# Storing one group of x1 in two cuts, with the first loads of the next stage between them

## The chip, the core and the metric

The kernel runs on one core of one Trainium2 chip, in one launch. The metric is the device time of that launch in microseconds (us), as the median of several runs. The engines of the core are named as in the profile: PE (TensorE), DVE (VectorE), ACT (ScalarE), POOL (GpSimd) and SP (SyncE). In this kernel SP does no arithmetic; it issues nearly all the transfers between the chip's memory and the on-chip memory.

## What is computed

The input x has 8 elements (B) of 8 channels, each 512 x 512 in float32. Two layers are applied, each with a residual. Cut to what matters:

```
# layer 0
x1 = x + spectral(gn(x))          # 2D Fourier modes of the subsampled x, 8 by 4 of them, mixed over channels
# layer 1
v   = gn(x1)                      # mean and variance over groups of 2 channels
cml = v                           # 15 steps of a lattice map
repeat 15 times:
    m   = 3.9 * cml * (1 - cml)
    cml = 0.85 * (0.7 * m + 0.3 * conv3x3_per_channel(m)) + 0.15 * v
cml = clip(cml, 1e-4, 1 - 1e-4)
nca = sigmoid(conv1x1(relu(conv3x3(v, 128 hidden))))
g   = sigmoid(conv1x1(relu(conv3x3([v, cml, nca], 8))))
out = x1 + g * cml + (1 - g) * nca
```

## The kernel before, in words

For every element the kernel keeps three planes in the chip's memory: `xn` (the normalised x1), `cml` and `nca`, with rows outermost and the 8 channels of a row next to each other (`[row, channel, 512]`, with a row of padding at the top, so that plane row 1 is image row 0).

**Layer 0** is the generator `layer0`. Its last part goes through the channels two at a time (a group): it adds the spectral part to a tile of x (128 partitions, four image rows in each), takes the statistics, and `close` normalises both tiles of the group on DVE (L414) and stores them into `xn` (L417, one DMA of 1024 KB for a channel). The store is put off by a tick with `later`. For element 0 the store also hands the tile's place back to the pool `sets` (`done_with`), and `e.stored` counts the channels.

**Layer 1** has three kinds of work, which for elements 1 to 7 run beside layer 0 of the next element:

- the lattice steps (`Half`, `convolve` L533, `settle` L588 and L594). The image rows lie in 5 sets of four slabs; every set has one tile of input for even steps (dE) and one for odd steps (dO), loaded from `xn` in four DMAs of 256 KB each (`Half.load`, L491), scaled on POOL (L526), and a state m, which begins as a square of dE on ACT (L513);
- the hidden rounds (`Hidden`). A round is four image rows. `load` (L616) fetches `cols`, 18 rows of all channels for four rounds, in one DMA of 512 KB, with two buffers. A round is a burst of matmuls (L633), a ReLU on ACT (L639) for one half and on DVE (L641) for the other; after two rounds `point` (L652) multiplies by the second matrix, and the result is copied out of PSUM into y by ACT (L659) for the first two rounds of four, and added to y by DVE (L661) for the other two. After four rounds the sigmoid (L665) is taken and y is stored into `nca` (L668, 256 KB). There is one buffer for y;
- the gates (`Gate`), which join x1, cml and nca.

The order of all this is written out by hand: `work` emits one slot of steps and rounds, and `keep_order` fixes the order of the source on every engine. The transfers are in one queue, SP's, in the order in which they are emitted, each with a wait for what it needs.

**Around the change.** Element 0's layer 0 has nothing beside it. When it is over, `tick(end=True)` runs what was put off, and two `e.hidden.load()` calls emit the loads of the first eight rounds. Then follow eight rounds (`FIRST_ROUNDS`) in four calls of `work`, each with two rounds. The first of them emits all loads of dE and dO for which there is room (`first.fetch`), the second, after its round, the next cols and, a tick later, the store of y. After these eight rounds the first lattice steps begin.

SP's order in the prologue is thus: four stores of x1 (channels 0 to 3), 16 loads of dE and dO (sets 0 and 1), four stores (channels 4 to 7), two cols, 24 loads of dE and dO (sets 2 to 4), one cols, the store of the first y, one cols, the store of the second y. Two cols loads reach down to plane row 33, that is the first 33 image rows, which lie in partitions 0 to 8 of the tiles of x1.

Of the kernel before, what the change touches and what calls it, by code (L numbers as in the profile page):

```python
# [41 lines left out]
P = 128  # L42
C = 8
N = 512
NS = N // 2
G = 4
# [74 lines left out]
def view(t, offset, dims):  # L121

    return bass.AP(tensor=t.tensor, offset=t.offset + offset, ap=[list(d) for d in dims])
# [3 lines left out]
def conv_layers(ctx: ExitStack, tc: tile.TileContext, a, out):  # L127
    nc = tc.nc
# [39 lines left out]
    def later(ticks, work):  # L168
        put_off.append((now[0] + ticks, work))

    def tick(end=False):
        now[0] += 1
        due = [w for at, w in put_off if end or at <= now[0]]
        put_off[:] = [] if end else [(at, w) for at, w in put_off if at > now[0]]
        for work in due:
            work()
# [122 lines left out]
    def group_stats(mv, n, bank):  # L299

        mean = sm.tile([P, n], F32, name=f"mean{n}")
        ps = bank[-1][:, 0]
        nc.tensor.matmul(ps[:, :n], avg, mv[:, :, 0], start=True, stop=True)
        nc.vector.tensor_copy(mean, ps[:, :n])
        var = sm.tile([P, n], F32, name=f"var{n}")
        nc.vector.tensor_tensor(var, mv[:, :, 0], mean, ALU.subtract)
        nc.vector.tensor_tensor(var, var, var, ALU.mult)
        nc.vector.tensor_tensor(var, var, mv[:, :, 1], ALU.add)
        yield LATER
        ps = bank[-1][:, 0]  # L310
        nc.tensor.matmul(ps[:, :n], avg, var, start=True, stop=True)
        std = sm.tile([P, n], F32, name=f"std{n}")
        nc.scalar.activation(std, ps[:, :n], AF.Sqrt, bias=eps)
        rstd = sm.tile([P, n], F32, name=f"rstd{n}")
        nc.vector.reciprocal(rstd, std)
        return mean, rstd, std

    def layer0(e, bank):
# [9 lines left out]
        for c in range(C):  # L328
            yield c
            xt = e.x[c]  # L330
# [76 lines left out]
        def close(g, mv):  # L407

            mean, rstd, std = yield from group_stats(mv, 1, bank)
            nc.vector.tensor_copy(means[:, 0, g : g + 1], mean)  # L410
            nc.vector.tensor_copy(means[:, 1, g : g + 1], std)
            for c in (2 * g, 2 * g + 1):
                xt = e.x[C + c]
                nc.vector.tensor_scalar(xt, xt, mean, rstd, ALU.subtract, ALU.mult)  # L414

                def store(c=c, xt=xt):
                    nc.sync.dma_start(  # L417
                        out=e.xn[1 : N + 1, c].rearrange("(p j) w -> p j w", j=4), in_=xt
                    )
                    e.done_with(C + c)  # L420
                    e.stored += 1

                later(1, store)

        def synthesis(ty, xt, st, half):
            ps, at = bank[-1], slice(2 * half, 2 * half + 2)
# [12 lines left out]
        for c in range(C):  # L439
            yield C + c  # L440
            ty, xt = ty_next, e.x[C + c]
            if c % 2 == 0:
                st = sm.tile([P, 2, 4, 6], F32, name="st1", bufs=2)
            synthesis(ty, xt, st[:, c % 2], 0)
            if closing:
                yield LATER
                next(closing)
                yield LATER
                next(closing, None)
                closing = None  # L450
            if c + 1 < C:
                yield
                ty_next = over_rows(c + 1)
            yield LONG
            synthesis(ty, xt, st[:, c % 2], 1)
            if c % 2:
                closing = close(c // 2, aggregate(st, 1))
# [217 lines left out]
    class Gate:  # L675
# [60 lines left out]
        def store(self):  # L736
            lo = self.first - self.r0
            nc.sync.dma_start(
                out=view(
                    out, self.e.b * C * N * N + self.first * N,  # L740
                    [[N, GR - lo], [N * N, C], [1, N]],
                ),
                in_=self.mix[C * lo : GR * C, 1],
            )
            shared.drop(self.mix)
# [110 lines left out]
    for i in range(3):  # L856
        xn = dram.tile([NP + 1, C, N], F32, name=f"xn{i}")
        cml, nca = (dram.tile([NP, C, N], F32, name=f"{name}{i}") for name in ("cml", "nca"))
        for plane in (xn, cml, nca):
            nc.scalar.dma_start(  # L860
                out=view(plane, 0, [[(NP - 1) * C * N, 2], [N, C], [1, N]]), in_=zrow
# [5 lines left out]
    e = Element(0)  # L867
# [13 lines left out]
        while e.stored >= C // 2 and len(e.first.loads) > 8 * (SETS - 2) and sets.free:  # L881
            e.first.load(nc.sync)
    tick(end=True)
    e.hidden.load()
    e.hidden.load()

# [29 lines left out]
    for b in range(B):  # L918
        e = elements[b]
# [95 lines left out]
```

## Time and profile before

| | us |
|---|---|
| median of 3 runs | 9992.99 |
| the runs | 9989.27, 9992.99, 10003.49 |
| the profiled execution, its own time | 9988.58 |
| its span | 9986.8 |
| PE busy (matmul) in the span | 9359.6, 94% |
| DVE busy | 5869.1, 59% |
| ACT busy | 4297.8, 43% |
| POOL busy | 1755.5, 18% |
| mean granted clock of PE | 0.983 |

The profile is of one execution. Times within it count from the start of the span. A row of the order of time gives the start, the length, the engine and line, the operation, what it writes and reads, how many such instructions are merged into the row, and in brackets the idle time before it and what ended that. An engine name with a q (SPq) means its queue, where DMAs are issued: the length is then that of the issuing, not of the transfer. A row of busy times by stretch gives from:to, the length, the busy time of PE, PE's weight loads, DVE, ACT and POOL (with the number of instructions), the granted clock of PE, the mean busy share of the 16 DMA engines and the GB/s that they moved. A transfer that goes on beyond its own record makes such a share come out a little over 1.

### The profile page before, as it was taken

What the parts mean: (1) busy time and instruction counts of PE and PEld (TensorE: products, weight loads), DVE (VectorE), ACT (ScalarE), POOL (GpSimd) and SP (SyncE); (2) the same over time, 40 slices, a digit from 0 to 9 for tenths busy, and PEclk for the clock granted to TensorE, in tenths of its full rate; (3) what the DMA queues carried; (4) which work ended last, traced back from release to release, by engine and by line L of the source; (5) the groups of instructions that cost most, each with busy time, mean ns of one, the idle gap of its engine ahead of it and who ended that gap; (6) DMA issues with size and microseconds to landing.
All of it is one profiled execution on the core that took longest, in us unless ns stands there. A gap on an engine that the chain in (4) does not pass through costs nothing. (4 is left out here: it accounts for less than half of the span.)

```text
span 9986.8 us, 353049 instructions
## 1 busy us (share of the span) xinstructions
PE 9359.6 (94%) x160496; PEld 4296.7 (43%) x160496; DVE 5869.1 (59%) x6067; ACT 4297.8 (43%) x4445; POOL 1755.5 (18%) x1406
## 2 busy tenths in 40 slices
PE   6999999899998999989999899999999899998999
PEld 2444444443444444444444444444434444444433
DVE  5665555665566655666556655566555565555555
ACT  2444444444444434444344443444434354344422
POOL 2010111103121031101312013120121202211212
PEclk9999999999999999999999999999999999999999
DMA  4241355447544565445665356552566526753688
GB/s 147 88 120 34 82 140 134 134 127 168 139 128 136 126 163 137 133 124 135 159 144 141 112 141 162 141 158 94 143 160 145 155 91 144 168 129 94 150 199 200
DMA packets 625562, 1353.48 MB, mean 136 GB/s; under 512 B 73066, under 2 KB 73194, under 8 KB 594050
## 3 DMA queue, kind: packets, MB, share of 16 engines
q1 hardware_dynamic: 621728, 1329.77, 52.0%
q8 instruction: 1261, 20.66, 0.9%
q14 instruction: 235, 1.93, 0.1%
q10 hardware_dynamic: 2338, 1.13, 0.0%
HBM read 992.27 MB, written 268.78 MB: 126 GB/s over the span
## 5 line engine op out<-in xcount | busy, mean ns | idle before, releaser
L533 PE MATMUL pair<-m,band 32*32 32x512 f32 x115200 | 4096.7, 605 | 200.2 <-issue 96.0
L594 ACT ACTIVATE m<-m 128x1024 f32<-128x1024 f32 x2240 | 2363.7, 1055 | 2795.7 <-DVE m L588 2674.2
L533 PEld LDWEIGHTS pair<-m,band 32*32 32x32 f32 x115200 | 2262.4, 103 | 1941.3 <-issue 970.0
L633 PE MATMUL pair<-cols,w_p 32*128 32x511 f32 (+1 forms) x24576 | 2866.2, 603 | 41.4 <-DMA cols<-xn 14.2
L588 DVE SCALAR_TENSOR_TENSOR m<-pair,dO 128x1024 f32<-128x1024 f32 x1280 | 1507.2, 1219 | 1478.0 <-PE pair L533 1294.2
L633 PEld LDWEIGHTS pair<-cols,w_p 32*128 32x128 f32 x24576 | 1270.8, 186 | 1651.0 <-issue 1123.3
L588 DVE SCALAR_TENSOR_TENSOR m<-pair,dE 128x1024 f32<-128x1024 f32 x1120 | 1319.1, 1219 | 1068.6 <-PE pair L533 878.3
L641 DVE TENSOR_SCALAR h<-pair,b_p 128x1024 f32<-128x1024 f32 x1024 | 1312.9, 1283 | 810.8 <-PE pair L633 803.3
L639 ACT ACTIVATE h<-pair,b_p 128x1024 f32<-128x1024 f32 x1024 | 1140.3, 1114 | 1043.4 <-PE pair L633 1043.0
L652 PE MATMUL pair<-h,w_u 128*32 128x512 f32 x8192 | 996.5, 598 | 136.4 <-DVE h L641 123.5
L726 POOL TENSOR_TENSOR mix<-mix 96x512 f32<-96x512 f32 x344 | 437.4, 1271 | 3757.9 <-ACT mix L724 3551.2
L703 PE MATMUL pair<-gin,w_g 128*32 128x511 f32 (+1 forms) x8256 | 964.1, 600 | 33.3 <-DMA gin<-nca 17.0
L708 POOL TENSOR_TENSOR mix<-mix 96x512 f32<-96x512 f32 x344 | 443.4, 1289 | 2050.6 <-DMA mix<-nca 1340.1
L598 POOL TENSOR_SCALAR dO<-dO 128x2048 f32<-128x2048 f32 x80 | 431.9, 5410 | 1225.6 <-DVE m L588 1225.5
L652 PEld LDWEIGHTS pair<-h,w_u 128*32 128x32 f32 x8192 | 249.4, 110 | 757.1 <-issue 384.0
L703 PEld LDWEIGHTS pair<-gin,w_g 128*32 128x32 f32 x8256 | 235.3, 110 | 711.2 <-issue 472.2
L665 ACT ACTIVATE y<-y,b_u 128x512 f32<-128x512 f32 x256 | 184.7, 721 | 808.0 <-DVE y L661 807.8
L731 DVE SCALAR_TENSOR_TENSOR mix<-mix,back 96x512 f32<-96x512 f32 x344 | 335.7, 976 | 148.5 <-POOL mix L726 148.5
L659 ACT COPY y<-pair 128x512 f32<-128x512 f32 x256 | 149.7, 585 | 605.1 <-PE pair L652 482.8
L713 DVE TENSOR_SCALAR mix<-pair,b_g 128x512 f32<-128x512 f32 x344 | 258.0, 750 | 251.6 <-PE pair L703 251.4
L720 PE MATMUL pair<-mix,w_g 128*32 128x512 f32 x2064 | 356.8, 593 | 9.6 <-DVE mix L713 7.8
L526 POOL TENSOR_SCALAR dO<-dO,base 128x512 f32<-128x512 f32 x320 | 237.0, 756 | 453.8 <-DMA dO<-xn 323.0
(86 smaller groups left out, 2643.8 us busy)
## 6 DMA issues: line engine op xcount, KB each, us to landing
gin<-xn SPq DMA_DIRECT2D x344, 384.0 KB
cols<-xn SPq DMA_DIRECT2D x256, 512.0 KB
x<-in_x SPq DMA_DIRECT2D x120, 1024.0 KB
gin<-cml SPq DMA_DIRECT2D x344, 320.0 KB
gin<-nca SPq DMA_DIRECT2D x344, 320.0 KB
dE<-xn SPq DMA_DIRECT2D x320, 256.0 KB
dO<-xn SPq DMA_DIRECT2D x320, 256.0 KB
mix<-xn SPq DMA_DIRECT2D x344, 192.0 KB
```

The source lines that it names most:

```text
L533: nc.tensor.matmul(ps[h // 2][32 * t : 32 * t + 32, h % 2], band[at, c0 + (t if step % 2 else h), dx], m[at, t, dx : dx + N], start=(n == ...
L588: nc.vector.scalar_tensor_tensor(u[:, at], ps[q], FLOOR, d[:, at], ALU.max, ALU.add)
L594: nc.scalar.square(u[:, at], u[:, at])
L598: nc.gpsimd.tensor_scalar(d, d, 0.5, None, ALU.add)
L633: nc.tensor.matmul(ps[g // 2][:, g % 2, lo:hi], w_p[p, dx, i % 2], self.cols[p, i // 2, at : at + hi - lo], start=(n == 0), stop=(n == 2), ...
L639: nc.scalar.activation(h[:, :2], ps[0], AF.Relu, bias=b_p)
L641: nc.vector.tensor_scalar(h[:, 2:], ps[1], b_p, 0.0, ALU.add, ALU.max)
L652: nc.tensor.matmul(ps[32 * g : 32 * g + 32], w_u[:, r % 4], h[:, g], start=(r == self.hs[0][0]), stop=(r == self.hs[-1][0]), tile_position ...
L703: nc.tensor.matmul(ps[32 * j : 32 * j + 32, lo:hi], gband[:, dx], gin[:, j, at : at + hi - lo], start=(n == 0), stop=(n == 2), tile_positi ...
L708: nc.gpsimd.tensor_tensor(d, d, ng, ALU.subtract)
L720: nc.tensor.matmul(ps[at], gpoint[:, at], mix[:, 3], start=True, stop=True, tile_position=(0, 32 * j),)
L726: nc.gpsimd.tensor_tensor(d, d, mix[: GR * C, 2], ALU.mult)
```

## The change

The put-off store of a group is now one function for both channels. For element 0 and the last group (channels 6 and 7) the store is cut at partition 12: first partitions 0 to 11 of both channels (48 image rows each), then the two cols loads, which stood after the end of layer 0, then partitions 12 to 127 of both channels (464 image rows each). In all other cases there is one cut, so the same two DMAs as before, with the places handed back after both of them.

```diff
-                def store(c=c, xt=xt):
-                    nc.sync.dma_start(
-                        out=e.xn[1 : N + 1, c].rearrange("(p j) w -> p j w", j=4), in_=xt
-                    )
+            def store():
+
+                cuts = (0, 12, P) if not e.b and g == G - 1 else (0, P)
+                for lo, hi in zip(cuts, cuts[1:]):
+                    for c in (2 * g, 2 * g + 1):
+                        to = e.xn[1 + 4 * lo : 1 + 4 * hi, c]
+                        nc.sync.dma_start(
+                            out=to.rearrange("(p j) w -> p j w", j=4), in_=e.x[C + c][lo:hi]
+                        )
+                    if lo == 0 and hi < P:
+                        e.hidden.load()
+                        e.hidden.load()
+                for c in (2 * g, 2 * g + 1):
                     e.done_with(C + c)
                     e.stored += 1
 
-                later(1, store)
+            later(1, store)
...
     tick(end=True)
-    e.hidden.load()
-    e.hidden.load()
```

## The prediction

> **What bounds the kernel now.** I read the page first: the span is 9986.8 us and TensorE (PE) is busy 94% of it, so the kernel is bound by PE almost everywhere, but the first of the 40 slices has PE at 6 tenths. The change touches only that slice. The page's chain of waits does not reach back to it, so I read the stretch from 120 to 200 us in order of time, queue by queue. Columns are: start in us, length, engine and line, operation, tiles, count, and in brackets the idle time before it with what ended it. First the queue of SyncE (SP), which issues all the DMAs here:
>
> ```profile
> 121.74 12.07 SPq L417 DMA_DIRECT2D xn<-x  x4
> 139.87 0.92 SPq L616 DMA_DIRECT2D cols<-xn  x2
> 140.83 1.89 SPq L491 DMA_DIRECT2D dE<-xn  x4
> ...
> 162.15 3.52 SPq L491 DMA_DIRECT2D dO<-xn  x4
> 166.73 0.38 SPq L616 DMA_DIRECT2D cols<-xn  x1
> 167.84 0.34 SPq L668 DMA_DIRECT2D nca<-y  x1
> 184.25 0.36 SPq L616 DMA_DIRECT2D cols<-xn  x1
> ```
>
> The last two of the four x1 stores are issued at 131.67 and about 133.3:
>
> ```profile
> 131.67 2.14 SPq L417 DMA_DIRECT2D xn<-x  x2
> ```
>
> Then SP stands until 139.87, because the first rounds' rows (cols) read what those stores write. Behind the two cols loads come 24 loads of dE and dO, one more cols, and only then the store of y into nca. Next PE and, for one line, ScalarE (ACT):
>
> ```profile
> 143.47 7.05 PE L633 MATMUL pair<-cols,w_p 32*128 32x512 f32 x48 [14.21 <-DMA cols<-xn]
> ...
> 171.64 3.70 PE L633 MATMUL pair<-cols,w_p 32*128 32x512 f32 x28
> 178.72 5.48 PE L633 MATMUL pair<-cols,w_p 32*128 32x512 f32 x20 [3.38 <-ACT y L659]
> 185.74 3.64 PE L652 MATMUL pair<-h,w_u 128*32 128x512 f32 x16 [1.54 <-ACT m L513]
> 189.31 7.45 PE L533 MATMUL pair<-m,band 32*32 32x512 f32 x192
> ```
>
> ```profile
> 178.08 0.58 ACT L659 COPY y<-pair 128x512 f32<-128x512 f32 x1 [8.67 <-DMA nca<-y]
> ```
>
> There are two gates. One is the start of the rounds, 143.47, held by cols. The other is 178.08: y has a single buffer, so the third pair of rounds cannot be copied out until the first y has been stored, and the fourth pair needs the PSUM bank that this copy empties. The lattice steps (L533) come after it in PE's fixed order. So the second gate, not the first, sets when the steps begin, and it is a DMA landing. Is that DMA late because it is issued late or because the queue is full? The busy times by stretch (last two columns: mean busy share of the 16 DMA engines, GB/s) answer it:
>
> ```profile
> 133.00:138.00 5.00, 0.00 (x0) 0.00 (x0) 0.99 (x4) 0.00 (x0) 1.49 (x2) 1.00 1.05 408
> 139.00:141.00 2.00, 0.00 (x0) 0.00 (x0) 0.00 (x0) 0.00 (x0) 0.00 (x0) 1.00 0.08 10
> 141.00:144.00 3.00, 0.53 (x4) 0.52 (x8) 0.00 (x0) 0.00 (x0) 0.00 (x0) 1.00 0.97 334
> 145.00:165.00 20.00, 16.88 (x144) 6.56 (x140) 5.82 (x5) 7.04 (x7) 2.80 (x6) 1.00 1.04 219
> 165.00:175.00 10.00, 8.42 (x76) 3.24 (x68) 2.92 (x3) 2.23 (x2) 2.70 (x4) 1.00 1.04 225
> 739.00:742.00 3.00, 3.00 (x99) 1.67 (x102) 0.18 (x1) 2.50 (x2) 2.64 (x5) 1.00 0.83 296
> ```
>
> From 141 to 175 the DMA engines are full, apart from the hole at 139 to 141 that SP's wait leaves. The nca store is at the end of that full queue.
>
> **What the Trainium skill says.** "DMA: Bandwidth & Descriptors", section "Why a DMA increments its semaphore by 16 and not by 1": a DMA issued from SP is spread over k engines, the largest number up to 16 that divides the outermost dimension of both sides, and these are the lowest-numbered ones. The trace agrees: in the last row above the cml stores of 24 to 28 partitions (13 on average by this rule, 13/16 = 0.81) keep 0.83 of the engines busy at 296 GB/s, where the 128-partition stores keep 1.05 busy at 408. The same page, "Queues, rings and completion order": one engine takes its descriptors in the order of the ring, so what is issued later waits behind what is queued on that engine. No row of before isolates this. "TensorE: Matmul & The Clock Gate", "The HAM clock gate": after an idle window of about 3.4 us the clock drops to a half, and a busy window brings it back. The trace shows that: PEclk is 0.50 from 180 to 190 after the 3.38 us of idle.
>
> **The change, part by part.** Only SP's order in the prologue differs; elements 1 to 7 keep theirs (store, store, then release).
>
> *Small stores ahead.* Partitions 0 to 11 of the two tiles, 48 rows of 2 KB each. 12 divides both 12 and 48, so k = 12 and each engine has 4 rows. They are issued where the full stores were, 131.67 and 133.3, and the queue ahead of them (the first two stores, 2.1 MB) is through at about 133. Before, SP went on at 139.87, some 1.2 us after the stores' traffic broke off (the 2 us row of nearly nothing begins at 139). Issue to first traffic was also about 1.3 us (139.87 to 141.1). So the last small store moves at about 134.6 and SP goes on at about 136.0.
>
> *Cols moved ahead.* 136.0 instead of 139.87, then the same 3.6 us to the first matmul (139.87 to 143.47): the rounds start at about 139.6, a gain of 3.9 us. It is not worth 10 us, as the 1.9 MB that pass behind might suggest, since the DMA queue stands empty while SP waits in either order. Of this gain nothing survives if the second gate does not move: PE would stop 3.9 us earlier and wait 3.9 us longer.
>
> *Rest of the stores behind cols.* 116 partitions, 464 rows of 2 KB, twice: 1.90 MB. The largest number up to 16 that divides both 116 and 464 is 4. So these two use four engines, and the same four. One engine gives 408/16 = 25.5 GB/s (128-partition stores) or 296/13 = 22.8 (cml stores); four give 91 to 102, and 1.90 MB take 18.6 to 20.8 us instead of 4.7. With cols moving from 137.3 to 139.9 (1.05 MB at 400 GB/s), these four are taken until 158.5 to 160.7. The two extra issues on SP (0.5 us each) are hidden behind this.
>
> *What is late next.* Everything behind has a share on those four engines. In the compiled order each DMA waits for one of eight completion semaphores in turn, so six loads go out freely, the seventh when the first rest has landed (about 151), the eighth when the second has (160 to 162). The other twelve engines finish their shares of the first seven loads and then stand idle. The four then owe seven shares of 64 KB, 0.46 MB at about 100 GB/s: 4.6 us, to 163.1 to 165.3. Before, the seventh load was through at 143.7 + 7 x 1.20 = 152.1 (262 KB at 219 GB/s, starting when cols were done). That is 11.0 to 13.2 us late. From here the sequence is as before, except that the twelve are one or two loads ahead, and the four alone do a share in 0.65 instead of 1.20 us: about 1 us comes back. The nca store lands 10 to 12 us later; I take 10.5, so ACT's copy comes at 178.1 + 10.5 = 188.6.
>
> *After the gate.* The squares of dE, the driving of dO on GpSimd and the first steps need loads that landed before nca, in both orders. The clock is the part that I cannot fix: PE ran 178.7 to about 191 at half speed, 5.48 us for 20 matmuls that at the rate of the others (5.43 for 48) would take 2.26. PE idles longer now and restarts in the same cold state; one window of 3.4 us more or less is worth 1.7 us of work, two 3.4. I take nothing, and keep plus or minus 3.4. Sum: +10.5, rounded to +10 for the rounding of both ends. Against the profiled execution's own 9988.58 us (its span 9986.8 and 1.8 around it) this makes 9998.6. That execution is 4.4 below the median of the three runs, 9992.99, which I forecast from: 10003.
>
> **The rivals.**
> *Spread evenly.* If the 116-partition stores use all 16 engines, they take 4.7 us. Then the DMA work is the same in another order, and only the hole differs: before it was 139 to 141.1 plus the end of 138; now the queue is nearly empty from 133.1 to 137.3. The loads begin at 139.9 + 4.7 = 144.6 instead of 143.7: +1 us, 9994. The cml row speaks against it.
> *The gate moves with the rounds.* If the nca store lands earlier with y, the 3.9 us arrive at the end: 9989. For it: y is ready 3.9 us earlier. Against it: ACT had finished y at 164.4 and SP issued the store at 167.84, behind 16 loads, with the engines full.
> *Slower by over 0.2%.* The place is the same rest stores, but on two engines or one: two take 37 to 42 us, so the nca store lands about 29 us late, 10022; one gives some 66, 10059. It decides from a rest of about 29 us on, that is from below 2.6 engines. For it: a dimension that is carried otherwise than 116 and 464 would have other divisors. Against it: the order of the compiled program shows 464 rows on the far side, and 4 divides both.
>
> **How the numbers follow.** Four engines 0.72, 9997 to 10010 (10 to 12 by the sum, 3.4 for the clock, a few for the median of three runs that span 14 us); spread evenly 0.12, 9990 to 9998; the gate moves 0.05; over 0.2% slower 0.11. 0.2% is 20 us, about what a measurement of this kernel can tell from no change. Range 9992 to 10013. Faster by over 0.2% 0.01, within 0.87, slower 0.12.
>
> **What would show it.** In the profile after: cols issued at about 136 and PE's first round at about 139.6; a DMA share near 4/16 somewhere between 147 and 158; the dE and dO issues stretched, with two long waits for the x1 stores at 151 and 161; ACT's copy at about 188 still ended by the nca store, with PE idle some 14 to 17 us before it instead of 3.38; the first L533 at about 199. If the share stays at 1.04 through 145 to 158 and the copy comes near 179, the step with four engines is wrong. If the copy is no longer ended by the nca store, the second gate is.

## The result, and the profile after

| | before | after |
|---|---|---|
| median (20 runs each) | 9990.17 us | 10009.37 us |
| lowest to highest | 9982.74 to 10015.66 | 9989.67 to 10032.20 |
| ratio of the times, after to before, 95% interval | | 1.0016, 1.0009 to 1.0023 |
| span of the profiled execution | 9986.8 us | 9996.6 us |
| copy of the third pair of rounds (ACT) | 178.08 | 191.87 |
| first lattice step (L533 before, L542 after) | 189.31 | 201.04 |

The changed kernel is slower by 9 to 23 us. The medians are 19.2 us apart, the two profiled executions 9.8. Lines after L414 have moved down by up to 9, the hidden rounds by 9 (L633 is L642, L659 is L668).

SP's queue in order of time, after:

```profile
121.86 11.83 SPq L422 DMA_DIRECT2D xn<-x  x4
136.18 0.91 SPq L625 DMA_DIRECT2D cols<-xn  x2
137.15 6.82 SPq L422 DMA_DIRECT2D xn<-x  x2
144.01 12.78 SPq L500 DMA_DIRECT2D dE<-xn  x4
...
182.09 0.38 SPq L625 DMA_DIRECT2D cols<-xn  x1
183.27 0.34 SPq L677 DMA_DIRECT2D nca<-y  x1
```

The cols loads do go out 3.7 us earlier. But two stores take 6.82 us merely to issue, where four took about 0.5 us each before, and the 24 loads behind them end their issue some 15 us later than before (182.09 against 166.73 for the cols load that follows them). PE and the copy on ACT:

```profile
139.65 6.84 PE L642 MATMUL pair<-cols,w_p 32*128 32x512 f32 x48 [10.27 <-DMA cols<-xn]
...
192.50 5.14 PE L642 MATMUL pair<-cols,w_p 32*128 32x512 f32 x20 [21.20 <-ACT y L668]
199.19 1.92 PE L661 MATMUL pair<-h,w_u 128*32 128x512 f32 x16 [1.54 <-DVE h L650]
201.04 6.58 PE L542 MATMUL pair<-m,band 32*32 32x512 f32 x192
```

```profile
191.87 0.59 ACT L668 COPY y<-pair 128x512 f32<-128x512 f32 x1 [26.49 <-DMA nca<-y]
```

PE starts 3.8 us earlier and then stands 21.20 us instead of 3.38, at the same place and for the same reason. Busy time by stretch (the last two columns are again DMA share and GB/s):

```profile
133.00:138.00 5.00, 0.00 (x0) 0.00 (x0) 0.59 (x2) 0.00 (x0) 1.77 (x3) 1.00 0.50 126
142.00:152.00 10.00, 8.47 (x76) 3.29 (x72) 2.57 (x2) 2.81 (x3) 0.00 (x0) 1.00 0.27 101
165.00:175.00 10.00, 5.55 (x44) 2.01 (x44) 1.89 (x2) 0.38 (x1) 2.81 (x6) 0.91 0.99 213
```

From 142 to 152 only about 4 of the 16 DMA engines are busy (0.27), at 101 GB/s. Before, the stretch from 145 to 165 us ran at 1.04 and 219.

### The profile page after: what moved, and what is told of

Same layout as the page of the kernel before. It is cut to its first block, busy times and chain, and to the rows that moved or that the text cites. A ratio compares the mean times of both kernels' runs of the same rounds, so it can differ in the third digit from the quotient of the medians.

```text
span 9996.6 us, 353055 instructions
## 1 busy us (share of the span) xinstructions
PE 9355.8 (94%) x160496; PEld 4301.1 (43%) x160496; DVE 5864.0 (59%) x6067; ACT 4298.8 (43%) x4445; POOL 1759.2 (18%) x1406
## 4 chain that ended last, share of the span: by engine, by line
PE 50%; DMA 5%; issue 4%; DVE 2%; POOL 1%; SPq 1%; ACT 1%; POOLq 0%; ACTq 0%; DVEq 0%
PE pair L542 23%; PE pair L642 15%; PE pair L712 5%; PE pair L661 5%; PE pair L729 2%; DVE h L650 1%; DMA dE<-xn 1%; DMA gin<-nca 1%; DMA mix<-nca 1%; DMA dO<-xn 1%; DVE m L597 1%; DMA cml<-m 0%; DVE mix L740 0%; DMA mix<-xn 0%; POOL dO L607 0%
## 5 line engine op out<-in xcount | busy, mean ns | idle before, releaser
L542 PE MATMUL pair<-m,band 32*32 32x512 f32 x115200 | 4095.5, 604 | 213.7 <-issue 107.8
L542 PEld LDWEIGHTS pair<-m,band 32*32 32x32 f32 x115200 | 2262.4, 103 | 1946.0 <-issue 983.3
L642 PE MATMUL pair<-cols,w_p 32*128 32x511 f32 (+1 forms) x24576 | 2864.8, 603 | 54.6 <-ACT y L668 21.2
L642 PEld LDWEIGHTS pair<-cols,w_p 32*128 32x128 f32 x24576 | 1275.1, 186 | 1663.2 <-issue 1120.9
L712 PE MATMUL pair<-gin,w_g 128*32 128x511 f32 (+1 forms) x8256 | 968.0, 602 | 30.4 <-DMA gin<-nca 15.4
L668 ACT COPY y<-pair 128x512 f32<-128x512 f32 x256 | 149.9, 585 | 628.3 <-PE pair L661 470.2
```

Of the source, the lines that this page charges most:

```text
L542: nc.tensor.matmul(ps[h // 2][32 * t : 32 * t + 32, h % 2], band[at, c0 + (t if step % 2 else h), dx], m[at, t, dx : dx + N], start=(n == ...
L642: nc.tensor.matmul(ps[g // 2][:, g % 2, lo:hi], w_p[p, dx, i % 2], self.cols[p, i // 2, at : at + hi - lo], start=(n == 0), stop=(n == 2), ...
L712: nc.tensor.matmul(ps[32 * j : 32 * j + 32, lo:hi], gband[:, dx], gin[:, j, at : at + hi - lo], start=(n == 0), stop=(n == 2), tile_positi ...
```

## The experiments

My theory: the rest of the stores, 116 partitions and 464 rows, runs on four engines, everything behind waits for these, and the store of the first y at the end of the queue hands the delay to PE. Rivals: the order itself, the two more DMAs, or stores mixed with loads make the queue slow; or the start of the rounds matters after all. The position of the copy and of the first lattice step in the profile is the sharper reading, since the end of one execution differs by 10 us and more from another of the same kernel. All ratios are to the kernel before on the same chip, with the 95% interval.

### The cut at 16, 10 and 15

```diff
-                cuts = (0, 12, P) if not e.b and g == G - 1 else (0, P)
+                cuts = (0, 16, P) if not e.b and g == G - 1 else (0, P)
```

and likewise with 10 and with 15. Order, number of DMAs and bytes in all stay; only the shapes change.

> The cut stands at partition 16 instead of 12, so the rest is 112 partitions and 448 rows, which 16 divides; order and number of the DMAs are those of the changed kernel. If the four engines are the cause: DMA share near 1 from 138 us on, no stretched issue on SP behind the rest, ACT's copy of y back at 178 to 180 (191.9 in the changed kernel, 178.1 before), time within 4 us of the kernel before. If the order (loads ahead of the rest), the two more DMAs or the mixing of stores with loads are the cause: the copy stays at about 190 and the time about 10 us or more over the kernel before.

> The cut stands at partition 10: the rest is 118 partitions and 472 rows, whose largest common divisor up to 16 is 2. Four-engine theory, with 82 ns for a row on one engine: 2 x 472 rows on two engines take 38.7 us, from 139.9 to 178.6; the copy of y follows 33 us after that end, as in the changed kernel, at about 211.6, 33.5 later than before; time some 30 us over the kernel before; DMA share 0.13 meanwhile. If the order or the mixing is the cause: the copy at about 192 as in the changed kernel.

> The cut stands at partition 15: the rest is 113 partitions and 452 rows, with no common divisor up to 16 but 1. Four-engine theory: 904 rows on one engine at 82 ns take 74 us, from 139.9 to 214; the copy of y at about 247, 69 later than before; time some 65 us over the kernel before; DMA share 0.06 meanwhile. If the order or the mixing is the cause: the copy at about 192.

| cut | rest: partitions | engines | rows for one engine in each store | copy of the third pair | first lattice step | ratio |
|---|---|---|---|---|---|---|
| none (before) | 128 | 16 | 32 | 178.08 | 189.31 | 1 |
| 16 | 112 | 16 | 28 | 177.85 | 187.41 | 1.0002 (0.9993 to 1.0012) |
| 12 (after) | 116 | 4 | 116 | 191.87 | 201.04 | 1.0016 (1.0009 to 1.0023) |
| 10 | 118 | 2 | 236 | 208.51 | 217.47 | 1.0034 (1.0020 to 1.0047) |
| 15 | 113 | 1 | 452 | 241.18 | 250.74 | 1.0071 (1.0056 to 1.0086) |

The copy follows the rows for one engine: from 116 to 452 in each of two stores it is 49.3 us later, 73 ns for each of the 672 rows more. The stretch behind the cols shows the engines directly, first with the cut at 16, then at 10, then at 15:

```profile
142.00:152.00 10.00, 8.47 (x68) 3.14 (x64) 2.57 (x2) 2.81 (x3) 0.00 (x0) 1.00 1.05 284
```

```profile
142.00:168.00 26.00, 21.30 (x192) 8.20 (x192) 8.39 (x7) 9.28 (x9) 0.00 (x0) 1.00 0.14 52
```

```profile
142.00:185.00 43.00, 26.35 (x216) 10.07 (x208) 9.67 (x8) 9.28 (x9) 0.00 (x0) 0.90 0.07 26
```

DMA shares of 0.14 and 0.07 are two engines and one; 52 and 26 GB/s are 26 each. The three expectations of the four-engine theory hold, but for two points. With the cut at 16 the first four loads behind the rest still took 1.2 to 2.5 us each to issue, where none was expected to be stretched. With the cuts at 10 and 15 the copies came 3 and 6 us sooner than expected. The rest stores ended where they were expected to (the eighth load, which waits for the second of them to land, goes out at 178.18 and 213.62; expected 178.6 and 214), so it is the 33 us from there to the copy that were too many. The order, the two more DMAs and the mixing of stores with loads are all in the kernel with the cut at 16, and there they cost nothing that shows. The third rival of the prediction, two engines or one, is thus real as a mechanism, but for other cuts than 12.

SP's own issues, first of the changed kernel, then with the cut at 10, then at 15 (the second rest store, and the first load behind it):

```profile
137.89 6.08 SPq L422 DMA_DIRECT2D xn<-x  x1
144.01 9.00 SPq L500 DMA_DIRECT2D dE<-xn  x1
```

```profile
136.52 14.36 SPq L422 DMA_DIRECT2D xn<-x  x1
150.93 18.42 SPq L500 DMA_DIRECT2D dE<-xn  x1
```

```profile
138.17 31.05 SPq L422 DMA_DIRECT2D xn<-x  x1
169.26 35.53 SPq L500 DMA_DIRECT2D dE<-xn  x1
```

The load behind stands in its own issue for 9.00, 18.42 and 35.53 us. That is 78 to 79 ns for each of the 116, 236 and 452 rows of one rest store: its issue ends about as long after the one before it as one engine needs for a whole store. So SP does not get past a DMA while the engines have more than a certain number of rows ahead of it still to move (the last section estimates how many).

### One piece more instead of another cut

```diff
-                cuts = (0, 12, P) if not e.b and g == G - 1 else (0, P)
+                cuts = (0, 12, 16, P) if not e.b and g == G - 1 else (0, P)
```

> The rest is cut once more, at partition 16: a piece of 4 partitions (16 rows, 4 engines, 4 rows each) and one of 112 partitions (448 rows, 16 engines), for both channels; so two DMAs more than in the changed kernel, everything else its own. If the number of rows that four engines have to carry is the cause: copy of the third pair at 178 to 180, DMA share near 1 from 138 us on, time within 5 us of the kernel before. If the number of DMAs or the move of the loads costs time: later than in the changed kernel (191.9).

The copy came at 178.97, the first lattice step at 188.40; ratio 1.0003 (0.9994 to 1.0011). Two DMAs more, and a few rows on four engines, cost nothing that shows: it is the number of rows on few engines that counts.

### The move alone undone

```diff
-                    if lo == 0 and hi < P:
-                        e.hidden.load()
-                        e.hidden.load()
...
     tick(end=True)
+    e.hidden.load()
+    e.hidden.load()
```

> The stores are cut at partition 12 as in the changed kernel, but the two cols loads stay behind all of them, so that the move alone is undone. If the gate of the lattice steps is the store of the first y behind the loads, and four engines are what delays it: PE starts its first round only at about 160 instead of 139.7, and yet the copy of the third pair comes at 190 to 195 as in the changed kernel (191.9), the first L533 at 199 to 204, time 10 to 20 us over the kernel before: the move buys nothing at the end. If the start of the rounds counts at the end: the copy and the first L533 some 20 us later than in the changed kernel, time 30 us or more over the kernel before.

PE's first round and first lattice step:

```profile
162.03 8.49 PE L639 MATMUL pair<-cols,w_p 32*128 32x512 f32 x48 [32.22 <-DMA cols<-xn]
...
200.49 6.58 PE L539 MATMUL pair<-m,band 32*32 32x512 f32 x192
```

The rounds start 22.4 us later than in the changed kernel, and the first lattice step comes 0.5 us earlier; the copy comes at 192.68. Ratio 1.0018 (1.0011 to 1.0025). Moving the loads ahead bought nothing at the end: in the changed kernel PE stands 21.20 us at the second gate, and the later start of the rounds is taken out of that stop. Here PE goes from its first round to the first step without a stop, in 38.5 us (37.7 in the kernel before with a place of its own for y, see below). So the start of the rounds and the second gate allow the first step at nearly the same time in this kernel, and a still later start would have cost time.

### A place of its own for the very first y

```diff
-                self.y = wk.tile([P, N], F32, tag="y", name="y", bufs=1)
+                self.own = None
+                if self.e.b or self.hs[0][0]:
+                    self.y = wk.tile([P, N], F32, tag="y", name="y", bufs=1)
+                else:
+                    self.own = shared.take([P, 4, N], "y0")
+                    self.y = self.own[:, 0]
...
+                    if own is not None:
+                        shared.drop(own)
```

This takes the second gate away. It was made on the kernel before, on the changed kernel, and on the one with the cut at 16.

> The kernel before with a place of its own for the very first y, so that the copy of the third pair of rounds does not wait for the store of the first y. If that store is the gate of the first lattice steps: PE has no 3.4 us hole at 175 and stays at full clock, the first L533 starts at 179 to 182 instead of 189.3, time 5 to 10 us under the kernel before. If the loads of dE and dO or something else is as late as that store: the first L533 stays at 187 or later and the time is the same.

> The changed kernel, four engines and all, with a place of its own for the very first y. If the store of the first y is the only way in which the late queue reaches PE: no stop of 21 us at 171, the first L533 at about 177 to 179 (201.0 in the changed kernel, 189.3 before, 180.9 in the kernel before with the same place for y). If the late loads of dE and dO are a gate too: the first L533 or one of the next three bursts waits for them, and the third burst (209.9 in the kernel before with that place for y) starts later than 210.

> The cut at partition 16 and a place of its own for the very first y: both gates moved. If the two gates are what the stage is held by: the 3.4 us by which the rounds start earlier with the cut now arrive, first L533 at 177 to 178 against 187.4 (cut 16 alone), 180.9 (that place for y alone) and 189.3 (before); third burst at about 206; 12 us under the kernel before at 230 us of the span, time 0 to 15 us under it. If the early start is lost again to a further gate: first L533 at 180 to 181, as with the place for y alone.

| | first round | first lattice step | third burst of steps | ratio |
|---|---|---|---|---|
| before | 143.47 | 189.31 | 218.58 | 1 |
| after | 139.65 | 201.04 | 229.32 | 1.0016 (1.0009 to 1.0023) |
| before, own place for y | 143.14 | 180.88 | 209.87 | 1.0004 (0.9993 to 1.0014) |
| after, own place for y | 139.99 | 176.90 | 216.00 | 1.0001 (0.9993 to 1.0010) |
| cut at 16, own place for y | 140.75 | 178.70 | 207.78 | 0.9990 (0.9981 to 0.9998) |

In all three the stop before the first step is gone, so the store of the first y was the gate. In the changed kernel the late queue then reaches PE at the next place, the cols of the ninth round:

```profile
176.90 6.58 PE L542 MATMUL pair<-m,band 32*32 32x512 f32 x192
191.47 5.64 PE L642 MATMUL pair<-cols,w_p 32*128 32x512 f32 x24 [8.00 <-DMA cols<-xn]
```

I had looked for a late dE or dO there; it was a late cols, which I had not named. So the store of the first y is the first place where the late queue reaches PE, and not the only one: the third burst is still 6.1 us later than in the kernel before with its own place for y.

With the cut at 16, the third burst is 10.8 us earlier than before. Against the kernel before with the place for y, its rounds start 2.4 us earlier, its first step comes 2.2 earlier and the third burst 2.1: once the second gate is gone, nearly all of the earlier start arrives. (The first step at 178.70 lies between the two expectations; the rounds started 1.0 us later than with the cut alone, 139.71.) Of the kernels tried this is the only one whose interval lies below 1, by 2 to 19 us; one such interval among eleven, ending so near 1, is weak evidence of a gain. The time to the end did not improve with the place for y alone, although its first step is 8.4 us earlier. Its interval, from 7 us under the kernel before to 14 over, just leaves out a gain of that size, so some of it seems to be given back later; the runs do not tell where.

### Another issuer for the rest

```diff
-                        nc.sync.dma_start(
+                        queue = nc.scalar if lo else nc.sync
+                        queue.dma_start(
```

and the same with `nc.gpsimd`.

> The changed kernel with the two rest stores issued from ScalarE's queue instead of SP's; same cut, same four engines, same bytes. If the loss is made by SP standing behind its own stores (issues of 6.1 and 9.0 us) and by loads queued in the same order on the four engines: the loads run beside the stores, the copy of the third pair comes at 179 to 185 instead of 191.9, though ScalarE now stands in its own issue for 10 to 15 us and delays the first rounds by as much. If the work on four engines costs the same whoever issues it: the copy stays at 189 to 193.

> The changed kernel with the two rest stores (116 partitions, 464 rows each) issued by GpSimd instead of SP; in GpSimd's order they stand ahead of the first driving of dO, so its work waits for them until 133. If the few engines come from how SP's queue splits a DMA, and GpSimd's queue splits the same shape more evenly: no stretch with a DMA share of 0.26, SP's issues of dE not stretched, the copy at 176 to 182. If the shape alone decides, whoever issues it: a DMA share of 0.26 for some 19 us from about 134 on, the cols landing later than in the changed kernel or the loads late as there, the copy at 185 or later.

From ScalarE's queue the copy came at 204.26; ratio 1.0029 (1.0016 to 1.0043). Both expectations missed, and the run is no test of them: ScalarE issued the rest before SP had come to its part, and the eight completion semaphores are shared by both queues, so that SP's loads of dO of set 1, which stand ahead of all this, waited for the rest stores to land. SP's waits:

```profile
SPq L501 <- DMA xn<-x: 37.6, 3, 24.6
```

From GpSimd the copy came at 185.25, 7.2 us later than before and 6.6 earlier than in the changed kernel, though the rounds started only at 150.76; ratio 1.0012 (1.0005 to 1.0019). The issues by line give 23.0 us to landing for a rest store, and the busy times by stretch show what ran beside it:

```profile
xn<-x POOLq DMA_DIRECT2D x2, 928.0 KB, 23.0
```

```profile
138.00:158.00 20.00, 7.24 (x40) 3.21 (x44) 1.28 (x1) 1.11 (x1) 2.74 (x5) 1.00 0.83 221
```

So the rest is still slow to land, but the loads ran beside it (0.83 of the engines, not 0.27). Neither expectation came as a whole: that no stretch at 0.26 appeared fits the first, while SP's stretched issues (7.73 us for the first four loads of dE) and the copy at 185.25 fit the second. This run changed the place of the stores and GpSimd's order as well, and how GpSimd's queue spread them was not separated from that.

## Why the prediction held

*The second gate.* "Of this gain nothing survives if the second gate does not move": shown. The copy is ended by the store of the first y before and after; undoing the move alone left the first step where it was (200.49 and 201.04; that the late rounds there just allow it is a coincidence), and taking the gate away removed the stop.

*The small stores and cols.* Forecast: cols at 136.0, rounds at 139.6. Measured 136.18 and 139.65.

*Four engines for the rest.* Forecast 18.6 to 20.8 us at 91 to 102 GB/s. Measured 96 to 101 GB/s with a share of 0.26 to 0.27, and SP's eighth load, which waits for the second rest store to land, went out at 161.7. The Trainium skill's rule on the number of engines ("DMA: Bandwidth & Descriptors", "Why a DMA increments its semaphore by 16 and not by 1") gave 16, 4, 2 and 1 for four shapes, and all four agree with the shares.

*What is late next.* Here one term was too small. Up to the end of the rest stores the forecast holds: the eighth load was to go out at 160 to 162. Then the four engines owe their shares of seven loads, for which I took 4.6 us at about 100 GB/s, that is 0.65 us for a share instead of 1.20. But 100 GB/s on four engines is the rate of the stores. The loads before ran at 219 GB/s on 16 engines, which is 1.20 us for a share. SP's order shows what it took. From the ninth load on, each waits for the load eight places ahead of it to land:

```profile
158.42 1.42 SPq L500 DMA_DIRECT2D dO<-xn  x2
161.74 0.30 SPq L500 DMA_DIRECT2D dO<-xn  x1
163.08 3.84 SPq L500 DMA_DIRECT2D dE<-xn  x4
167.89 3.41 SPq L500 DMA_DIRECT2D dO<-xn  x4
172.45 4.05 SPq L500 DMA_DIRECT2D dE<-xn  x4
```

So the first load had landed at 163.08 and the ninth at 172.45, 1.17 us for each. Seven shares at this pace take 8.2 us, 3.6 more than forecast. The copy came 13.8 us later than before where 10.5 were forecast, 3.3 more (191.87 against 188.6), and this term accounts for about all of it. Nor were the four ever alone: each load that lands lets SP issue another one to all sixteen, and from 162 to 166 us the DMA share was 0.75 to 0.81. Whether four engines alone would be quicker at loads, no run shows.

"Six loads go out freely" while the rest runs was wrong as well. SP stood in its own issues (6.08 and 9.00 us), so the first load was not through its issue before 153.0, and the other twelve engines stood empty meanwhile. But the seventh load was through its issue at 159.84, before the second rest store had landed (161.74): the four engines had all seven shares before them when they came free. So SP's standing cost the twelve engines time, and the gate none that the trace shows.

*After the gate.* The clock gave a little back. From the copy to the first step it was 11.23 us before and 9.17 after, as PE came back to full speed sooner (it restarted at 178.72 and had a granted clock of 0.50 until about 191 before, from 192.50 to about 197 after; the second matrix took 3.64 us before and 1.92 after). I had taken nothing for it and kept 3.4 either way. So the first step is 13.8 - 2.1 = 11.7 us later, as the two rows say, where I had 10.

*The sum.* Forecast 9998.6 for the profiled execution, with the 1.8 us around its span; measured 9996.6 + 1.8 = 9998.4. That agreement is luck, closer than the method: 11.7 us at the first step had become 9.8 at the end, and in another profiled execution the difference to before moved by 26 us between the first step and the end (the kernel before with its own place for y: 8.4 earlier at the first step, 17.6 later at the end of the span). Against the median, 10003 was forecast, 10 over the three runs before, and 10009.4 measured, 19.2 over the twenty runs before. The interval of 9 to 23 us holds both the 10 and the 11.7 of the first step; whether anything behind the prologue adds to them is not shown. Of the rivals, "spread evenly" is what the cut at 16 made, and "the gate moves with the rounds" happened nowhere without the place for y. For two engines and one the prediction had the first store of y about 29 and 66 us late; with the cuts at 10 and 15 the copy came 30.4 and 63.1 us late.

## What to carry to other kernels

A cut through a transfer is also a choice of its shape, and the shape decides how many of the 16 DMA engines carry it: look at the outermost dimension of both sides of every piece, and cut so that each piece divides by 16 (here at 16 instead of 12, which takes the loss away and alone brings no gain that shows). Take the rate of a transfer from a row of the same kind: here loads took nearly twice as long on an engine as stores of the same size. Before moving a load ahead, find the last gate of the stage, not the first: here the loads came 4 us earlier and the stage waited for a store at the end of the same queue. A slow transfer in a shared queue is paid by everything issued behind it, and the place where it is paid can be far from it.

## What I had not expected of the hardware

A DMA on few engines keeps the issuing queue busy: a load behind a store with 116, 236 or 452 rows for one engine took 9.00, 18.42 and 35.53 us to issue, against 0.3 to 0.6 us for such a load before. In all three kernels the second rest store had landed 8.7 to 8.8 us after the end of that issue (the eighth load, which waits for it, goes out at 161.74, 178.18 and 213.62). As an estimate, at 82 ns for a row (35.44 us for the 432 rows by which the cuts at 10 and 15 differ), that is about 107 rows for each of its engines, and somewhat fewer if the time from the last row to the landing is taken off: SP got past the load when some 100 rows ahead of it were left.
